# A fused three-layer transformer on one core: batch 0's q and k a tick earlier in the lead-in, and the modulations of two layers given out in smaller pieces

## The chip, the cores and the metric

The kernel runs on one core of a Trainium2 chip. A core has five engines that work side by side, each with its own queue of instructions that it takes in order: TensorE (PE in the profile; its weight loads are shown apart as PEld), VectorE (DVE), ScalarE (ACT), GpSimd (POOL) and SyncE (SP), which here issues nearly all transfers. An engine stops at an instruction until the instructions that it depends on, on other engines or in the DMA queues, are done, and everything behind it in its queue waits as well. The metric is the device time of one execution in microseconds.

## The reference

32 sequences ("batches") of 128 tokens with 144 channels, and one condition vector of 144 for each, pass through four layers:

```python
x = _L0_cond_ref(x, cond, ...)   # attention (q and k normalised per head), MLP
x = _L1_cond_ref(x, cond, ...)   # x + (z R - z) U^T, z = x U
x = _L2_cond_ref(x, cond, ...)   # attention, MLP
x = _L3_cond_ref(x, cond, ...)   # attention, mixture of 4 experts, top 2
```

Layers 0, 2 and 3 have 16 heads of 9 channels. Their normalised input is modulated, `ln(x) * (1 + scale) + shift`, and the result of attention and of the MLP is multiplied by a gate before it is added to x. Shifts, scales and gates come from the condition: `silu(c) @ w_mod + b_mod`, 144 to 6 x 144, a matrix for each of the three layers. Layer 0 also normalises q and k over the 9 channels of each head:

```python
q = _ln(q, g_q); k = _ln(k, g_k)      # mean and variance over 9 channels, then a learnt factor
attn = softmax(q @ k^T * 9 ** -0.5)
```

Layer 1 needs U, the orthogonal factor of a QR decomposition of P (144 x 64), and for each batch R = expm(A), where the 64 x 64 skew matrix A is filled from `silu(cond) @ W.T + b`. Neither depends on x.

## The kernel before

The three attention layers are numbered 0, 1 and 2 in the code (the rotation by U and R is done between 0 and 1). A fixed schedule, written out by hand, sets the order of all instructions: a loop over *ticks* from -6 on, and in each tick a row of named places, *gaps*: a, e, t, first half of the scores, stats, b0, b, den, pre1, second half of the scores, c, y1, y2, y3, d, z. In tick b of layer 0 the first scores of batch b are computed, in tick b + 1 its softmax weights, in tick b + 2 its sums and its projection. `put(tick, gap, f)` lays a piece of work into a gap; `fill(tick, gap)` gives it out. Ticks -6 to -1 are the lead-in. The kernel uses eight PSUM banks for what TensorE writes; one is kept for the attention outputs, and `bank()` hands out the other seven in rotation, so a matmul can wait for the engine that reads what the bank held seven banks ago.

Around the change lie these pieces:

- `modulations(n)` (L263 to L283): shifts and scales of layer n for all batches, 40 small matmuls into one bank (8 with 128 output rows, c < 4, and 32 with 32 rows, at L274) and four copies on DVE (L278 to L281) into modM and modR. `ln_T` (L652 to L655) transposes a normalised batch and applies modM and modR on ACT.
- `layer_gates(n)` (L285 to L300): the gates of layer n, four matmuls (L291), a copy on ACT (L296) and two writes to DRAM by SP (L298). `load_gates` (L305) brings them back, spread over 128 partitions, once per four batches.
- `first_gates` (L1178): layer_gates(0), then the loads of the last layer's modulation weights into the place that layer 0's held. `without_means` (L1170 to L1176): DVE takes the mean over each head out of the q and k weights, in place.
- Layer 0's q and k, batch by batch: `qk0_project` (L686, L687 on TensorE, a copy and a square on ACT, L741, L742), `qk0_variance` (a sum on DVE, L747; scaling on POOL, L748), `qk0_guess` and three `qk0_newton` (an inverse square root, L754 to L767; on DVE for batch 0, on POOL else), `qk0_divide` (DVE, L771) and `qk0_T` (four transposes, L783, and three copies on ACT, L786 to L788, into qT and kT, which the scores read).
- `prep_qr`: the QR decomposition, 64 columns one after another. Each column is a loop through the engines: TensorE spreads a row (L327), ACT squares and copies it (L338, L340), POOL takes a root (L339), DVE makes the reflection (L342 to L349) and applies it to the matrix `at` (L353), which the next column's matmul reads. `prepare_qr` gives out one column per tick in the lead-in and two per tick afterwards.
- `prep_expm`: the matrix exponential as a generator of many steps. Before: modulations and gates of layer 1 (one step), of layer 2 (one step), then the first half of A (matmuls L414 with the weights W4, copy on ACT L420), its transposition (`ps_at`, L429, and a product on DVE, L434), the second half, its transposition, the row sums and the scaling, the powers, the series and the squarings. Each half of A reads four tiles of W4; the second four are loaded (L189) into the same places once the first half has been computed. A branch (L585, L586) follows the first four squarings: further ones are computed only if a norm asks for it, which it does not here. All engines go through the branch.
- `prepare_expm` (L1208): gives out one step of `prep_expm` in gap z of tick -2, and from tick 0 on one in gap b and one in gap z of each tick.

## Time and profile before

| | us |
|---|---|
| three runs | 1311.20, 1311.47, 1315.63 (median 1311.47) |
| profiled execution | 1311.55 |
| its span, first to last instruction | 1309.8 |
| TensorE busy | 1264.6 (97%) |
| DVE / ACT / POOL busy | 799.4 / 833.1 / 701.9 |
| scores of batch 0 start | 40.47 |
| the branch | 323 |

A line of the profile's order of time gives start, duration, engine, source line, operation, the tiles written and read, shapes and count, and in brackets how long the engine had been idle and what ended that. Matmuls overlap, so their durations are longer than the distance from one to the next; an f32 matmul appears as two records. PEq, DVEq, SPq are the sequencers of the engines. Windows give the busy time of PE, PEld, DVE, ACT and POOL in a stretch, then the TensorE clock that was granted (1.00 is full), the mean share in which the DMA engines were busy, and GB/s.

### The profile page before, as it was taken

The page shows a single profiled execution, that of the slowest core. Times are in us where ns is not written, and L with a number is a line of the kernel's source. Part 1 is how long each engine was busy: PE and PEld are TensorE (multiplying, and loading weights), DVE is VectorE, ACT ScalarE, POOL GpSimd, SP SyncE. Part 2 cuts the span into 40 slices and gives each one's busy share as a digit, 9 for nine tenths or more (in the row PEclk, how much of TensorE's full clock was granted, in tenths as well). Part 3 has the DMA queues.
Part 4 walks back from the last instruction along what each step waited for, and adds up shares of the span by engine and source line. Part 5 has one row for each costly group of instructions (what it writes and reads, how often), then busy time and mean ns, then how long its engine had stood idle before and what let it go on. Part 6 is the DMA issues. An engine that isn't in the chain of part 4 may idle for free.

```text
span 1309.8 us, 35666 instructions
## 1 busy us (share of the span) xinstructions
PE 1264.6 (97%) x14180; PEld 924.2 (71%) x14180; DVE 799.4 (61%) x2516; ACT 833.1 (64%) x1832; POOL 701.9 (54%) x1691
## 2 busy tenths in 40 slices
PE   6889898999989999999999999999999999999997
PEld 5678686787776667667677767767676767677665
DVE  5698888876864456666666666646464646454322
ACT  2567768678757566777767777665656565555431
POOL 5667777765744444445545454746464646351632
PEclk9999999999989999999999999999999999999999
DMA  8200000000003000000110000200000000000000
GB/s 231 62 2 21 20 2 20 20 3 22 20 2 134 19 11 21 11 20 20 36 29 20 20 11 11 76 11 19 11 20 11 19 11 19 11 19 2 19 10 10
DMA packets 21671, 34.43 MB, mean 26 GB/s; under 512 B 2304, under 2 KB 12448, under 8 KB 21248
## 3 DMA queue, kind: packets, MB, share of 16 engines
q1 hardware_dynamic: 20848, 31.70, 8.1%
q8 instruction: 114, 1.87, 0.6%
q10 hardware_dynamic: 656, 0.42, 0.2%
q14 instruction: 53, 0.43, 0.1%
HBM read 29.65 MB, written 2.47 MB: 25 GB/s over the span
## 4 chain that ended last, share of the span: by engine, by line
PE 71%; DVE 2%; ACT 1%; POOL 0%; issue 0%; POOLq 0%; DVEq 0%
PE ps_h L665 19%; PE ps_f L1109 10%; PE ps_s L853 7%; PE ps_qk L665 6%; PE ps_w L853 6%; PE ps_o L880 5%; PE ps_f L974 5%; PE ps_pj L944 3%; PE ps_v L665 2%; PE ps_f L1114 1%; PE ps_o L812 1%; PE ps_cw L1097 1%; DVE nm L858 1%; PE ps_hT_m L652 1%; PE ps_hT_m L653 1%; PE ps_z L1006 1%
## 5 line engine op out<-in xcount | busy, mean ns | idle before, releaser
L858 DVE TENSOR_REDUCE nm<-ps_s 128x4 f32<-128x512 f32 x384 | 246.2, 682 | 90.1 <-PE ps_w L853 68.4
L865 ACT ACTIVATE pr<-ps_w 128x512 f32<-128x512 f32 x384 | 208.6, 595 | 104.0 <-PE ps_w L853 102.5
L853 PE MATMUL ps_s<-kT,qT 32*128 32x256 f32 x1536 | 227.8, 404 | 0.7 <-ACT kT L788 0.6
L853 PE MATMUL ps_w<-q,kT 32*128 32x128 f32 x3072 | 228.2, 282 | 0.0
L853 PEld LDWEIGHTS ps_w<-q,kT 32*128 32x128 f32 x3072 | 193.4, 187 | 9.8 <-issue 6.2
L968 ACT ACTIVATE hid<-ps_h 128x512 f32<-128x512 f32 (+1 forms) x224 | 119.5, 591 | 100.4 <-PE ps_h L665 99.9
L853 PEld LDWEIGHTS ps_s<-kT,qT 32*128 32x128 f32 x1536 | 134.5, 184 | 30.0 <-issue 8.9
L665 PE MATMUL ps_h<-hM_m,mlps 128*128 128x512 f32 x304 | 144.0, 607 | 0.0
L1118 DVE SCALAR_TENSOR_TENSOR acc<-ps_f,cw,acc 128x144 f32<-128x144 f32 x128 | 46.6, 365 | 152.3 <-PE ps_f L1114 73.5
L930 POOL TENSOR_TENSOR x_sb<-x_sb,res_a 128x144 f32<-128x144 f32 x96 | 47.1, 490 | 147.1 <-DVE res_a L933 146.4
L880 PE MATMUL ps_o<-pr,vaug 128*32 128x128 f32 x3072 | 104.1, 276 | 0.0
L880 PEld LDWEIGHTS ps_o<-pr,vaug 128*32 128x32 f32 x3072 | 78.1, 109 | 32.5 <-PE ps_w L853 18.9
L665 PEld LDWEIGHTS ps_h<-hM_m,mlps 128*128 128x128 f32 x304 | 53.3, 189 | 67.6 <-issue 66.6
L731 POOL TENSOR_SCALAR kT<-kT,cst 128x512 f32<-128x512 f32 x40 | 62.4, 1565 | 61.5 <-ACT kT L718 60.5
L974 PE MATMUL ps_f<-mlps,hid 128*128 128x144 f32 x640 | 94.8, 296 | 0.0
L974 PEld LDWEIGHTS ps_f<-mlps,hid 128*128 128x128 f32 x640 | 83.5, 193 | 7.6 <-issue 3.4
L865 ACT ACT_TABLE_LOAD x57 | 73.1, 1283 | 6.5 <-PE ps_w L853 5.7
L626 POOL TENSOR_SCALAR rs_m_a<-mv_m_a 128x2 f32<-128x2 f32 x81 | 15.6, 193 | 114.4 <-DVE mv_m_a L624 86.0
L655 ACT ACTIVATE hM_m<-ps_hT_m,modM 128x128 f32<-128x128 f32 x96 | 44.7, 465 | 50.5 <-PE ps_hT_m L653 50.4
L965 ACT ACT_TABLE_LOAD x58 | 74.4, 1283 | 1.0
L1109 PEld LDWEIGHTS ps_f<-pair,hid 128*128 128x128 f32 x512 | 66.9, 190 | 8.4 <-issue 7.7
L1109 PEld LDWEIGHTS ps_f<-mlps,hid 128*128 128x128 f32 x512 | 66.7, 190 | 8.2 <-issue 6.9
(324 smaller groups left out, 2931.1 us busy)
## 6 DMA issues: line engine op xcount, KB each, us to landing
gates<-gates SPq DMA_DIRECT2D x48, 288.0 KB, 3.5
x_sb<-in_x SPq DMA_DIRECT2D x8, 288.0 KB, 9.4
out_x<-x_sb SPq DMA_DIRECT2D x8, 288.0 KB, 2.5
mlps<-in_L_mlp SPq DMA_DIRECT2D x2, 1000.0 KB, 5.8
pair<-in_L_mlp SPq DMA_DIRECT2D x1, 1800.0 KB, 9.7
mlps<-in_L_mlp SPq DMA_DIRECT2D x1, 1800.0 KB, 8.2
pow<-in_W SPq DMA_DIRECT2D x4, 320.0 KB, 6.8
mlps<-in_L_wmod SPq DMA_DIRECT2D x4, 290.0 KB, 4.8
```

The lines of the kernel that those rows point to most:

```text
L665: nc.tensor.matmul(ps, x, y, start=k == 0, stop=k == 1)
L731: eng.tensor_scalar(o, k, m, None, ALU.mult)
L853: nc.tensor.matmul(o, x, y, start=True, stop=True)
L858: nc.vector.tensor_reduce(nmv[:, at0 : at0 + 2, ONE : ONE + 2], view.rearrange("p (r t k) -> p r t k", t=2, k=T), AX.X, ALU.max, negate=True,)
L865: nc.scalar.activation(pr[:, 4 * e : 4 * e + 4, :].rearrange("p s q -> p (s q)"), view, AF.Exp, scale=SCALE,)
L880: nc.tensor.matmul(po[rows4(j), t, :], v[:, 4 * j + 2 * t + r, :], prs[j // 2][:, 4 * (j % 2) + 2 * r + t, :], start=r == 0, stop=r == 1,)
L930: nc.gpsimd.tensor_tensor(x_sb[:, b, :], x_sb[:, b, :], t, ALU.add)
L965: nc.scalar.activation(t, half, AF.Gelu_apprx_tanh)
L968: nc.scalar.activation(hid[:n, i], ps[:n], AF.Gelu_apprx_tanh)
L974: nc.tensor.matmul(ps, hid[:, at0, i, :], w2[:, m, :], start=m == 0, stop=m == NFC - 1)
L1109: nc.tensor.matmul(ps[:, 0, :], hid[:, at0 + m, i, :], w2[:, at0 + m, :], start=m == 0, stop=m == 3)
L1118: nc.vector.scalar_tensor_tensor(acc, ps[:, 0, :], w, acc, ALU.mult, ALU.add)
```

## The change

The lead-in of layer 0 is ordered anew, and the step generator's first steps are cut smaller and given out at more places.

- `modulations(n)` computes its two parts one after the other, each into a bank of its own and each followed by its two copies; it is a generator now, with a step for each part. `prep_expm` has six steps for layers 1 and 2 (two parts and the gates each) where it had two.
- `prepare_expm` gives out nothing in the lead-in any more. In ticks 0 and 1 it gives out a step in each of the gaps b0, b, c, y2 and z; from tick 2 on in b and z, as before. Ten steps are therefore given out by the end of tick 1: the six above, the first half of A (tick 1, b), its transposition (c), the second half (y2) and its transposition (z). Before, that point was reached in tick 2, b. From tick 2 on every step of the exponential stands one gap earlier than before, the branch among them (tick 23, b, where it stood in tick 23, z).
- Batch 0's q and k are projected in tick -4 instead of -3, guessed and refined in tick -3 (on DVE, as before), divided at the end of tick -3 and transposed in tick -2.
- `first_gates` moves from tick -4 to tick -2, `without_means` from the end of tick -4 to gap t of tick -5.
- The scaling in `qk0_variance` goes to DVE for batches 0 to 3 and stays on POOL for the others.

```diff
     def modulations(n):
         w = w_mods[n]
-        mm = const.tile([128, 4, B], F32, name=f"modM{n}")
-        mr = const.tile([128, 4, B], F32, name=f"modR{n}")
-        ps = bank([128, 8, B], f"ps_mod{n}")
-        for c in range(8):
-            at0 = (c % 4) * (CM + 32)
-            for r in range(1 if c < 4 else 4):
-                m, at1 = (CM, at0) if c < 4 else (32, at0 + CM)
-                for k in range(2):
-                    rows = slice(0, KH + k)
-                    nc.tensor.matmul(
-                        ps[32 * r : 32 * r + m, c, :], w[k][rows, at1 : at1 + m], csT[rows, k, :],
-                        start=k == 0, stop=k == 1,
-                    )
-        nc.vector.tensor_copy(mm[:, :2, :], ps[:, :2, :])
-        nc.vector.tensor_scalar_add(mm[:, 2:, :], ps[:, 2:4, :], 1.0)
-        nc.vector.tensor_copy(mr[:, :2, :], ps[:, 4:6, :])
-        nc.vector.tensor_scalar_add(mr[:, 2:, :], ps[:, 6:8, :], 1.0)
-        modM.append(mm)
-        modR.append(mr)
+        for part, mods in enumerate((modM, modR)):
+            t = const.tile([128, 4, B], F32, name=f"mod{'MR'[part]}{n}")
+            ps = bank([128, 4, B], f"ps_mod{n}_{part}")
+            for c in range(4):
+                at0 = c * (CM + 32) + part * CM
+                m = 32 if part else CM
+                for r in range(4 if part else 1):
+                    for k in range(2):
+                        rows = slice(0, KH + k)
+                        nc.tensor.matmul(
+                            ps[32 * r : 32 * r + m, c, :], w[k][rows, at0 : at0 + m], csT[rows, k, :],
+                            start=k == 0, stop=k == 1,
+                        )
+            nc.vector.tensor_copy(t[:, :2, :], ps[:, :2, :])
+            nc.vector.tensor_scalar_add(t[:, 2:, :], ps[:, 2:, :], 1.0)
+            mods.append(t)
+            yield
...
         for n in (1, 2):
-            modulations(n)
+            yield from modulations(n)
             layer_gates(n)
             yield
...
-    def qk0_variance(s):
+    def qk0_variance(s, eng):
         va = small.tile([128, 32], F32, tag="qkv", name=f"qkv_{s}", bufs=2)
         nc.vector.tensor_reduce(va, st[s].pop("sq"), AX.X, ALU.add)
-        nc.gpsimd.tensor_scalar(va, va, 1.0, EPS, ALU.mult, ALU.add)
+        eng.tensor_scalar(va, va, 1.0, EPS, ALU.mult, ALU.add)
...
-        if prep_expm and (tick >= 0 and gap in ("b", "z") or (tick, gap) == (-2, "z")):
+        if prep_expm and tick >= 0 and gap in (("b0", "b", "c", "y2", "z") if tick < 2 else ("b", "z")):
             said = next(prep_expm, 0)
...
                 if layer == 0:
-                    put(t0 + i - 3, "c", qk0_project, s)
-                    put(t0 + i - 3, "z", qk0_variance, s)
-                    put(t0 + i - 2, "e", qk0_guess, s)
-                    if s == 0:
+                    early = s == 0
+                    put(t0 + i - 3 - early, "c", qk0_project, s)
+                    put(t0 + i - 3 - early, "z", qk0_variance, s, nc.vector if s < 4 else nc.gpsimd)
+                    put(t0 + i - 2 - early, "e", qk0_guess, s)
+                    if early:
                         for gap in "bbc":
-                            put(-2, gap, qk0_newton, s, nc.vector)
+                            put(-3, gap, qk0_newton, s, nc.vector)
+                        put(-3, "z", qk0_divide, s)
+                        put(-2, "b0", first_gates)
+                        put(-2, "b", qk0_T, s)
                     else:
                         for gap in ("b", "c", "y2"):
                             put(t0 + i - 2, gap, qk0_newton, s)
-                    put(t0 + i - 1, "b", qk0_divide, s)
-                    put(t0 + i - 1, "c", qk0_T, s)
+                        put(t0 + i - 1, "b", qk0_divide, s)
+                        put(t0 + i - 1, "c", qk0_T, s)
...
-    put(-5, "b", modulations, 0)
-    put(-4, "b", first_gates)
-    put(-4, "z", without_means)
+    put(-5, "b", lambda: list(modulations(0)))
+    put(-5, "t", without_means)
```

## The prediction

> **What bounds the kernel now.** I read the page's table of engines and its 40 slices first, then the windows of the first 90 us, then the order of time on TensorE, DVE and the DMA queue from 10 to 84 us, last the waits around the branch at 323 us. All numbers are us of the one profiled execution: span 1309.8, time 1311.55 (1.75 outside the span); the median of the three runs is 1311.47, so a sum made on the execution stands for the median as well. Three runs spread over 4.4 us, so 0.5%, 6.6 us, is about what can be told from no change.

> ```profile
> PE 1264.6 (97%) x14180; PEld 924.2 (71%) x14180; DVE 799.4 (61%) x2516; ACT 833.1 (64%) x1832; POOL 701.9 (54%) x1691
> ...
> PE 71%; DVE 2%; ACT 1%; POOL 0%; issue 0%; POOLq 0%; DVEq 0%
> ```

> TensorE is busy nearly all the time. The chain that ended last can be followed back to 323.15, the branch, and is TensorE throughout, so what the start of the program loses or gains is carried to the end. The windows (x counts; the last columns are granted clock, DMA share, GB/s) show where the edited stage is bound:

> ```profile
> 35.00:40.00 5.00, 2.96 (x9) 2.41 (x10) 1.69 (x7) 1.20 (x3) 4.07 (x15) 1.00 0.20 62
> 40.00:45.00 5.00, 5.00 (x38) 4.23 (x36) 3.62 (x14) 2.33 (x9) 3.82 (x13) 1.00 0.01 2
> 55.00:60.00 5.00, 4.76 (x71) 3.41 (x65) 4.86 (x12) 4.23 (x14) 4.09 (x15) 1.00 0.99 234
> 60.00:70.00 10.00, 9.93 (x146) 6.52 (x140) 7.51 (x25) 5.89 (x18) 5.72 (x19) 1.00 0.03 8
> 70.00:80.00 10.00, 6.99 (x97) 5.36 (x97) 9.17 (x35) 5.05 (x17) 6.15 (x18) 0.94 0.01 2
> ```

> Up to 40 us TensorE has holes; in 40 to 70 (ticks 0, 1 and most of 2) it is full; in 70 to 80 DVE is the bound. In order of time:

> ```profile
> 33.40 0.42 PE L652 MATMUL ps_hT_a<-cst,xh_a 128*128 128x128 f32 x1
> 37.04 1.09 PE L783 MATMUL ps_qkT<-cst,qkn 128*128 128x128 f32 x4 [3.01 <-DVE qkn L771]
> 40.47 1.50 PE L853 MATMUL ps_s<-kT,qT 32*128 32x256 f32 x8
> 42.98 0.27 PE L652 MATMUL ps_hT_a<-cst,xh_a 128*128 128x128 f32 x1
> ...
> 54.41 0.56 SPq L189 DMA_DIRECT2D wt<-in_W  x1
> ...
> 60.63 0.11 PEld L414 LDWEIGHTS ps_a<-wt,csT 72*32 72x32 f32 x1 [0.98 <-DMA wt<-in_W]
> ...
> 77.00 0.51 PE L327 MATMUL ps_qr<-at,cst 128*128 128x145 f32 x2 [1.78 <-DVE at L353]
> ...
> 323.29 0.73 PE L944 MATMUL ps_pj<-L_wproj,oT 128*128 128x144 f32 x4 [1.07 <-DVEq L586]
> ```

> and the windows behind the wait at 77.00, with the granted clock third from the end:

> ```profile
> 78.00:79.00 1.00, 1.00 (x22) 0.81 (x17) 0.96 (x4) 0.18 (x2) 0.79 (x4) 0.90 0.00 0
> 79.00:80.00 1.00, 1.00 (x8) 0.78 (x7) 0.86 (x4) 0.62 (x2) 0.96 (x3) 0.50 0.00 0
> ...
> 82.00:83.00 1.00, 1.00 (x7) 0.67 (x7) 0.90 (x5) 0.47 (x3) 0.47 (x2) 0.90 0.00 0
> ```

> The reader sees: the scores of batch 0 start at 40.47; TensorE ran at half speed until then (the same transpose takes 0.42 at 33.40 and 0.27 at 42.98, though the granted clock reads 1.00); the second product of the exponential (L414) already waits 0.98 for its weights W4; an idle of 1.78 is followed from 78.8 to 82.2 by a granted clock of 0.50; and the branch costs TensorE 1.07.

> **The change part by part.**

> *1. Lead-in.* Layer 1's modulations and gates leave it (26.45 to 32.75, 6.3 at half speed), and batch 0's q and k chain runs a tick earlier, but it now lies on DVE between two steps of the QR, which is the loop of the lead-in. Walking the new order with the rows of before: tick -5 keeps its times. The centring of the weights (L1170 to L1176, 18.91 to 21.37, 2.46) moves ahead of its QR step: 10.5 to 12.9, its weights having landed at 9.0 (issued 4.34, 4.7 to landing); the QR step then ends 14.7, under the modulations of layer 0, which hold TensorE to 15.3. Tick -4: q and k of batch 0 stand where the first gates stood, 17.2 to 19.3; ACT squares to 20.1, DVE's variance to 20.75, guess and statistics to 21.6, QR step to 23.35. Tick -3: three Newton steps on DVE (27.16 to 29.79, 2.63) and the division (0.45) end at 26.4; the next QR step waits behind them and ends 28.65, not 27.2. Tick -2 on TensorE: QR 23.4, first gates to 26.5, then the transposes of batch 0, q and k of batch 1 to 29.8. Tick -1: QR on DVE 32.3 to 34.05. So QR of tick 0 starts at 34.1 and the scores 0.63 later (39.84 to 40.47), at 34.7: **-5.75**. Ends: -7 if one QR turn (3.6 to 4.4) shrinks to its chain, -3 if a queue adds a wait in two ticks.

> *2. What comes back in tick 0.* The 40 matmuls of layer 1 and its four gate matmuls (counted before splitting into records) cost what layer 2's cost at full speed, 43.20 to 46.68: **+3.48**, on an engine without holes there. Six steps instead of two, but the same matmuls and DVE copies (0.23 and 0.21 each, beside TensorE); one more bank each, no instruction.

> *3. POOL and DVE at tick 0.* POOL must finish batch 1's Newton steps (3.83 for three, behind the statistics chain) before QR's square root: 38.1, 3.4 after the scores; in before 1.2 after. DVE's maxima and with them the banks of the second scores come about 0.8 late: **+0.8** (0 to 2). The variance's scaling for four batches goes from POOL (0.22) to DVE (0.18 by the same shape's row): nothing, DVE idles 3.93 before 40.83.

> *4. The W4 loads.* This is the largest loss. In before the two halves of the exponential's input stand a tick apart (tick 0 and tick 1, gap z). In after, five steps of tick 0 and one of tick 1 go to modulations and gates, and both halves fall into tick 1, gaps b and y2. The second half's weights overwrite the first's, so their four loads are issued when the first is done (51.74) and the last is there at 60.63: 8.89 later, with the DMA engines at 0.99 share and 234 GB/s, so by bandwidth. Between the halves TensorE will have QR 0.60, scores 1.34, transposes 0.49, q and k 0.97, ps_at 1.21: 4.61. It waits 4.28 in place of the 1.12 by which the second half is now longer (59.50 to 62.47 against 49.89 to 51.74): **+3.15** (0 if other waits fill it, 4.3). Behind the waiting matmuls stand the maxima's transpose (L812), so DVE's q and the next tick's weights. The second ps_at (L429) now follows at once and waits for ACT's copy of 0.59: **+0.6**. On SP the last gate writes stand ahead of the W4 loads as before; their data is ready 2 earlier (ACT's copy behind the exponentials, 4 into tick 1; the first half ends 6 into it), so they add nothing. The first gates' own transfers on SP (two writes, two weight loads of 290 KB, 24.03 to 26.25) move to about 27 to 29.5 and, with 4.8 to landing, are there at 34, some 10 before the modulations that read them: nothing.

> *5. Clock.* TensorE will idle 1.1 (at half speed) to 2.5 (at full) before tick 0 and 4.28 in tick 1. The nearest row is the idle of 1.78 and the 3.4 at 0.50 behind it, half of which is lost: 1.7. I take **+1.7** twice (each from 0; the first up to 6.8, see the second rival).
> [...]

> *6. The branch.* The expm chain ends one step earlier, and the branch moves from gap z to gap b of tick 23. There TensorE is done at 314.4, and DVE's last instruction ahead of the branch (qkn, 316.04 + 0.49) and its own load and compare (about 0.8) end at 317.3: 2.9 of idle in place of 1.07, **+1.8**. Ends 0 and 3.4 (TensorE's compare-and-branch alone lasts 3.40, covered now by matmuls). The other steps of the chain change places between b and z, two to a tick as before; bound +-2, taken as 0.

> Sum: -5.75 + 3.48 + 0.8 + 3.15 + 0.6 + 3.4 + 1.8 = +7.5. 1311.55 + 7.5 = **1319.0**.

> **The rivals.** (a) *DVE, not TensorE, sets ticks 0 to 3; not slower.* For it: DVE has 9.17 of 10 in 70 to 80, and TensorE idles 1.14, 1.78 and 0.38 there and loses 1.7 by the clock, 5.0 in all. Then items 2 and 4 and the second clock loss (8.9) hide: 1310.1. It decides once DVE has no idle of its own at the start of tick 2; in before it idles 2.11 at 62.0 to 64.15, which speaks against it. If the first clock loss and the branch are free too (3.5) it ends at 1306.6; if item 3 (0.8) and the half clock of 79 to 82 (1.7) go as well, at 1304.1, and with the lead-in's far end at 1302.8.
> (b) *Half speed lasts through tick 0.* For it: TensorE stayed at half speed from 10 to 40 us in before, dense as it was. The three pieces of modulations and gates (5.9 at full speed) and first scores and values (2.5) take 1.81 times as long (6.3 against 3.48): 6.8 in place of 1.7, 1324.1. Against it: 26.5 to 33 is dense with full matmuls in the new order, and in before 2.9 of such (37.04 to 39.9) came just ahead of full speed.
> (c) *The lead-in gives less*, since QR waits behind the Newton steps twice: -3, 1321.7.

> **How the numbers follow.** Forecast 0.46, (a) 0.34 (some 0.3 of that in its low end), (b) and (c) together 0.20. The forecast's own range is 1314 to 1325 and lies above 1318.1 in seven cases of ten: 0.32 slower, 0.14 same. (a) gives 0.10 faster, 0.21 same and, with the upper ends of clock and branch, 0.03 slower; (b) and (c) are slower. Slower 0.55, same 0.35, faster 0.10. The range 1306 to 1327 leaves out the low end of (a) and the upper tail of (b), some 0.16.

> **What would show it.** First ps_s near 34.7 (item 1; over 38 refutes it); a wait of L412 on the load of W4 near 4 in tick 1 (item 4); granted clock 0.50 behind it or matmuls at 0.42 in tick 0 (item 5, b); start of tick 3's scores some 5 to 6 later than 72.55 (items 1 to 5; at or before 72.55 speaks for (a)); an idle near 2.9 at the branch (item 6). The prediction is wrong if that wait is short, or if TensorE's idle of 70 to 84 is gone.

## The result and the profile after

The changed kernel takes 1327.32 us (median of 4 runs, 1325.94 to 1334.47), the kernel before 1311.34 on the same chip (4 runs, 1308.31 to 1315.63): a ratio of 1.0118, 95% interval 1.0081 to 1.0156. It is slower, by 1.2%. The profiled execution has a span of 1324.0 and a time of 1325.94, 14.1 and 14.39 more than before; the working below is on these two executions. The forecast was 1319.0 with a range of 1306 to 1327: the sign holds, the size is about half of what was measured (7.5 for 14.39 in the profiled execution and 15.5 by the ratio), and the median lies at the upper end of the range, 0.3 above it.

From here on, lines of the changed kernel's file behind the modulations are two lower than in the kernel before (L414 is now L412, L858 is L856).

The page of the changed kernel, engines and granted clock in 40 slices of 33 us:

```profile
PE 1271.1 (96%) x14180; PEld 928.6 (70%) x14180; DVE 799.5 (60%) x2520; ACT 832.4 (63%) x1832; POOL 698.6 (53%) x1687
...
PEclk8789998999999999999999999999999999999999
```

The first slices are below 9. The first slice of the kernel before reads 9, which tells nothing: its record of the clock begins at 41.2 (last section), while of the two transposes of a batch the second starts 0.21 after the first at 33.40 and 0.11 after it at 42.98. The windows of the changed kernel (us from the start, busy time of PE, PEld, DVE, ACT, POOL with instruction counts, then granted clock, DMA share, GB/s):

```profile
35.00:40.00 5.00, 5.00 (x24) 3.99 (x22) 1.31 (x8) 0.55 (x3) 3.92 (x16) 0.50 0.00 0
40.00:45.00 5.00, 5.00 (x80) 4.44 (x80) 3.16 (x12) 1.24 (x4) 2.24 (x8) 0.51 0.00 0
50.00:55.00 5.00, 5.00 (x101) 4.17 (x101) 3.37 (x18) 2.33 (x5) 1.80 (x5) 0.67 0.04 11
60.00:70.00 10.00, 8.53 (x77) 3.48 (x70) 4.00 (x12) 3.65 (x11) 2.46 (x9) 1.00 0.64 162
70.00:80.00 10.00, 8.63 (x132) 6.58 (x132) 8.70 (x29) 6.00 (x18) 6.12 (x20) 1.00 0.01 2
```

In 35 to 45, the first part of tick 0, TensorE is busy throughout and runs at a clock of 0.50; in 60 to 70 it waits while the DMA engines are at 0.64. In order of time on TensorE (start, length, line, tiles; in brackets the idle time before it and what ended it):

```profile
27.06 1.11 PE L781 MATMUL ps_qkT<-cst,qkn 128*128 128x128 f32 x4 [0.48 <-DVE qkn L769]
...
34.49 0.76 PE L325 MATMUL ps_qr<-at,cst 128*128 128x145 f32 x2 [2.14 <-DVE at L351]
35.19 2.08 PE L851 MATMUL ps_s<-kT,qT 32*128 32x256 f32 x8
...
42.69 0.42 PE L650 MATMUL ps_hT_a<-cst,xh_a 128*128 128x128 f32 x1
...
57.17 0.62 PE L412 MATMUL ps_a<-pow,csT 72*32 72x512 f32 x2
57.18 0.62 PE L412 MATMUL ps_a<-hid,csT 72*32 72x512 f32 x1
57.19 0.62 PE L412 MATMUL ps_a<-wt,csT 72*32 72x512 f32 x1
...
63.23 1.04 PE L412 MATMUL ps_a<-pow,csT 72*32 72x512 f32 x2
64.78 1.04 PE L412 MATMUL ps_a<-pow,csT 72*32 72x512 f32 x2 [0.51 <-DMA pow<-in_W]
66.14 1.05 PE L412 MATMUL ps_a<-hid,csT 72*32 72x512 f32 x2 [0.32 <-DMA hid<-in_W]
67.41 0.62 PE L412 MATMUL ps_a<-wt,csT 72*32 72x512 f32 x1 [0.22 <-DMA wt<-in_W]
...
69.25 0.33 PE L810 MATMUL ps_nm<-cst,nm 128*128 128x128 f32 x1
69.99 1.16 PE L427 MATMUL ps_at<-cst,hid 128*64 128x64 f32 x32 [0.42 <-ACT hid L418]
...
86.76 0.82 PE L325 MATMUL ps_qr<-at,cst 128*128 128x145 f32 x2 [2.06 <-DVE at L351]
...
330.90 0.48 PE L325 MATMUL ps_qr<-at,cst 128*128 128x145 f32 x2 [3.22 <-PEq L584]
```

The wait of qkT in the lead-in, 3.01 before, is 0.48, and batch 0's scores start at 35.19 (40.47 before). Then the scores last 2.08 and a transpose 0.42; at a clock of 1.00 they last 1.13 (at 45.02) and 0.27 (at 56.86). The second half of the exponential's products (63.23 to 69.25) lasts 6.02 in place of 2.97, with its bracketed waits all on the loads of W4. Those waits add up to only 1.05. The rest is lost because products no longer run side by side: in the first half four start within 0.02 of each other (57.17 to 57.19), in the second the first three start one by one, at 63.23, 64.78 and 66.14, as their tiles land. The branch costs TensorE 3.22 in place of 1.07. The lag of the changed kernel against the kernel before, taken at the maxima's transpose of each tick (ps_nm), is 0.90 in tick 0, 9.95 in tick 1, 8.86 in tick 2, 9.44 in tick 10, 13.30 in ticks 17 to 22, 16.89 in tick 23, 15.9 in ticks 25 to 27 and 14.7 from tick 29.

### The profile page after: what moved, and what is told of

Read it like the earlier page. It is cut to its first block, busy times and chain, and to the rows that moved or that the text cites. A ratio compares the mean times of both kernels' runs of the same rounds, so it can differ in the third digit from the quotient of the medians.

```text
span 1324.0 us, 35670 instructions
## 1 busy us (share of the span) xinstructions
PE 1271.1 (96%) x14180; PEld 928.6 (70%) x14180; DVE 799.5 (60%) x2520; ACT 832.4 (63%) x1832; POOL 698.6 (53%) x1687
## 4 chain that ended last, share of the span: by engine, by line
PE 70%; DVE 3%; ACT 1%; POOL 0%; issue 0%; POOLq 0%; DVEq 0%
PE ps_h L663 19%; PE ps_f L1107 9%; PE ps_s L851 7%; PE ps_qk L663 6%; PE ps_w L851 6%; PE ps_o L878 5%; PE ps_f L972 5%; PE ps_pj L942 3%; PE ps_v L663 2%; PE ps_f L1112 1%; PE ps_o L810 1%; DVE nm L856 1%; PE ps_cw L1095 1%; PE ps_z L1004 1%; PE ps_hT_m L651 1%; PE ps_hT_m L650 1%
## 5 line engine op out<-in xcount | busy, mean ns | idle before, releaser
L856 DVE TENSOR_REDUCE nm<-ps_s 128x4 f32<-128x512 f32 x384 | 246.4, 683 | 95.6 <-PE ps_w L851 73.9
L851 PE MATMUL ps_s<-kT,qT 32*128 32x256 f32 x1536 | 231.3, 409 | 0.6 <-ACT kT L786 0.6
L878 PEld LDWEIGHTS ps_o<-pr,vaug 128*32 128x32 f32 x3072 | 78.0, 109 | 32.3 <-PE ps_w L851 18.9
L624 POOL TENSOR_SCALAR rs_m_a<-mv_m_a 128x2 f32<-128x2 f32 x81 | 15.5, 191 | 114.6 <-DVE mv_m_a L622 86.2
```

Source lines behind the costliest of these rows:

```text
L851: nc.tensor.matmul(o, x, y, start=True, stop=True)
L856: nc.vector.tensor_reduce(nmv[:, at0 : at0 + 2, ONE : ONE + 2], view.rearrange("p (r t k) -> p r t k", t=2, k=T), AX.X, ALU.max, negate=True,)
L878: nc.tensor.matmul(po[rows4(j), t, :], v[:, 4 * j + 2 * t + r, :], prs[j // 2][:, 4 * (j % 2) + 2 * r + t, :], start=r == 0, stop=r == 1,)
```

## The experiments

All were compared with the kernel before on the chip where they ran; its median was 1310.88 (13 runs) for the lead-in, pieces, own-places and fill runs, 1312.64 (13 runs) for the three with wide operands and the branch run, 1312.01 (29 runs) for the next three (everything taken away, fillers alone, first combination) and 1312.77 (17 runs) for the last. "At tick 2" means the position of that tick's ps_nm against the kernel before, in the profiled executions.

### Half the change: the lead-in alone, the pieces alone

The lead-in run has the new lead-in, but gives out a layer's modulations and gates in one step at the old places; the pieces run has the old lead-in with the pieces at five places.

```
e3_lead (against the changed kernel)
-            yield from modulations(n)
+            list(modulations(n))
...
-        if prep_expm and tick >= 0 and gap in (("b0", "b", "c", "y2", "z") if tick < 2 else ("b", "z")):
+        if prep_expm and (tick >= 0 and gap in ("b", "z") or (tick, gap) == (-2, "z")):
```

```
e4_pieces (against the changed kernel; qk0_variance, qk0_newton, qk0_divide and qk0_T likewise)
-                    put(t0 + i - 3 - early, "c", qk0_project, s)
+                    put(t0 + i - 3, "c", qk0_project, s)
...
-    put(-5, "t", without_means)
+    put(-4, "b", first_gates)
+    put(-4, "z", without_means)
```

> The changed kernel with only its lead-in order kept: modulations and gates of layers 1 and 2 are one step each again, the first in tick -2, gap z, and steps come in gaps b and z as before. Theory (the loss comes from what the smaller pieces move into ticks 0 and 1: the W4 wait, half clock there, the branch at gap b): no such wait, branch at gap z, scores of batch 0 at 39 to 42, time 1309 to 1315. Rival (the reordered lead-in itself costs, by QR behind the Newton steps and by clock): scores at 43 or later, 1318 or more.

> The changed kernel with the old lead-in order put back (q and k of batch 0 in ticks -3 to -1, first gates in tick -4, centring of the weights at the end of tick -4) and the pieces in five gaps kept. Theory: the W4 wait of about 4, half clock in ticks 0 and 1 and the branch at gap b are all there: 1322 to 1330. Rival (the new lead-in order is what costs): 1309 to 1315.

Measured: lead-in alone 1308.35 (10 runs), ratio 1.0003 (0.9967 to 1.0039); pieces alone 1331.44, ratio 1.0155 (1.0108 to 1.0201). Both times lie just outside the theory's ranges (0.65 below and 1.4 above) and far from the rival's. The lead-in costs nothing that can be told, the pieces cost all. What they cost is seen in the windows of the pieces run:

```profile
50.00:55.00 5.00, 5.00 (x103) 4.44 (x105) 2.39 (x14) 1.45 (x5) 0.92 (x3) 0.80 0.05 11
55.00:60.00 5.00, 5.00 (x29) 3.95 (x26) 3.19 (x11) 2.25 (x4) 2.92 (x9) 0.50 0.03 7
60.00:65.00 5.00, 5.00 (x25) 1.42 (x27) 0.00 (x0) 1.82 (x5) 0.00 (x0) 0.50 0.00 0
65.00:70.00 5.00, 5.00 (x36) 3.73 (x38) 1.29 (x2) 2.82 (x9) 2.46 (x9) 0.50 0.86 218
```

From 53.0 to 70.0 the clock is halved, though TensorE has not waited: it is busy 5.00 of 5.00 in each window, the one ahead of the half clock included. My explanation of item 5, idle time, cannot be the cause here.

### The wait for W4 taken away

The second half of W4 gets places of its own (four of the tiles hid, and rotU) and is loaded behind the x tiles, so nothing has to be waited for.

```
-        wt = mat(f"wt{c}", ("pow3", "pow4", "even_lo", "odd_lo")[c % 4])[:KP]
+        tags = ("pow3", "pow4", "even_lo", "odd_lo", "w4_4", "w4_5", "w4_6", "w4_7")
+        wt = mat(f"wt{c}", tags[c])[:KP]
...
-            if t == 0:
-                for c in range(4, 8):
-                    load_W4(c)
             yield
```

> The changed kernel with places of their own for the second half of W4 (the MLP's hidden tile and the tile of the rotated U, unused until later), loaded behind the x loads at the start, so that nothing waits for the first half. Theory: no wait on W4, the second half takes 1.9 in place of 6.0, tick 2 starts 4.2 earlier than in the changed kernel, time 1321 to 1324. Rival (the wait only takes the place of DVE waits in ticks 2 and 3): tick 4 within 1 of the changed kernel, 1325 to 1328.

Measured: 1327.14, ratio 1.0122 (1.0072 to 1.0173); nothing gained, the theory's 1321 to 1324 is missed. In its trace the wait is gone, in order of time on TensorE:

```profile
69.08 0.62 PE L424 MATMUL ps_a<-hid,csT 72*32 72x512 f32 x2
...
70.41 0.60 PE L424 MATMUL ps_a<-rotU,csT 73*32 73x512 f32 x2
70.94 0.33 PE L819 MATMUL ps_nm<-cst,nm 128*128 128x128 f32 x1
```

The second half takes 1.86, but it starts at 69.08 in place of 63.23: its windows show why.

```profile
55.00:60.00 5.00, 5.00 (x23) 3.13 (x25) 1.61 (x4) 1.84 (x6) 1.30 (x5) 0.50 0.21 64
60.00:65.00 5.00, 5.00 (x38) 2.50 (x30) 0.00 (x0) 1.14 (x4) 1.19 (x4) 0.50 0.01 3
```

The clock, halved from 51.7 to 55.1 in the changed kernel, stays halved from 51.0 to 68.0 here. The 4.2 that the wait gives free go there. So the run does not say that the wait was harmless; it says that in this execution another loss of the same size took its place.

### What halves the clock

Four runs go after it. The fill run puts filler matmuls (the identity against itself, 128 by 128, results not read) into TensorE's waits ahead of tick 0. The wide run leaves the waits and changes the modulations and gates: the condition vectors are repeated four times, so that the modulations M stream 128 columns and the gates hold 128, in the same number of matmuls; the extra results are not read. The third does both, the fourth puts the wide operands into the lead-in run.

```
e5_fill
+    put(-3, "z", warm, 6)
+    put(-1, "z", warm, 9)

e6_wide
+    csW = pp.tile([KH + 1, 2, 4 * B], F32, name="csW")
+    csT = csW[:, :, :B]
...
-                            ps[32 * r : 32 * r + m, c, :], w[k][rows, at0 : at0 + m], csT[rows, k, :],
+                            ps[32 * r : 32 * r + m, c, :], w[k][rows, at0 : at0 + m], csW[rows, k, :wide],
...
-                    psg[:, c, :], csT[rows, k, :], w[k][rows, MODC + c * C : MODC + (c + 1) * C],
+                    psg[:, c, :], csW[rows, k, :], w[k][rows, MODC + c * C : MODC + (c + 1) * C],
```

The third run, e7_widefill, has both sets of lines; the fourth, e8_leadwide, is e3_lead with the lines of e6_wide.

> The changed kernel plus 15 matmuls of the identity with itself, 128x128, into the attention output's bank, which nothing reads then: 6 at the end of tick -3 and 9 at the end of tick -1, where TensorE idles 3.07 and 2.14. Theory (half clock in tick 0 follows from that idle and costs most of what the sum missed): granted clock 1.00 from about 31 to 45, the maxima's transpose of tick 0 at 46 instead of 50.55, time 1320 to 1323.5. Rival (the work moved into tick 0 costs by itself, clock or not): within 1.5 of the changed kernel's 1326 to 1327, or slower by the added 2.

> The changed kernel with the condition vectors repeated four times side by side: the modulations M stream 128 columns (32 before) and the gates hold 128 columns (32 before) on TensorE; the extra results are not read. The number of matmuls is the same, and a 128-column matmul lasts 0.11 in the traces, like the 32-column ones (0.45 for 4 at full speed). Theory 'array use': the clock is halved behind a stretch of some 3.4 in which the matmuls fill little of TensorE's array, whether it waits or runs small matmuls; then the half clock of 38.0 to 44.85 and of 51.68 to 55.09 in the changed kernel goes or shrinks, worth 2.5 to 4.5, at 1322.5 to 1325 (the wait of 2.14 ahead of tick 0 stays, so 34.6 to 38.0 may stay at half). Theory 'idle' (item 5: the clock is halved by TensorE's waits alone): no change, 1326.5 to 1328.

> The wide operands and the fillers of the fill run together (6 and 9 filler matmuls of 128 by 128 in TensorE's waits of ticks -3 and -1). Theory 'array use': with neither the wait nor the small matmuls ahead of and in tick 0, the half clock of 34.6 to 44.85 goes as a whole, 5 to 6.5 in all against the changed kernel: 1320.5 to 1322.5, while fillers alone gave 1328.92 and the wide operands alone less. Theory 'idle': as the fill run, 1327 to 1330.

> The lead-in run (changed lead-in; modulations and gates of a layer in one step as before) with the wide operands. Its half clock of 34.0 to 37.4 follows 3.4 of modulations and gates without any wait, that of 44.2 to 51.05 another such stretch. Theory 'array use': both go, worth 2.5 to 4 against the lead-in run's 1308.35: 1304 to 1306, faster than the kernel before by 0.3 to 0.5%. Theory 'idle': no change, 1307.5 to 1309.5.

Measured: fill 1328.92 (ratio 1.0136, 1.0087 to 1.0184); wide 1326.01 (1.0115, 1.0068 to 1.0162); both 1325.83 (1.0105, 1.0067 to 1.0143); lead-in with wide operands 1308.89 with the kernel before at 1312.64 (0.9977, 0.9948 to 1.0006). As times, all four miss the range of their theory, and the fill run and the lead-in run with wide operands end in that of the rival. By the time alone the wide operands gain nothing in the lead-in run either (1308.89 with them, 1308.35 without, on different chips). What decides is in the traces, one execution of each. The fill run, in order of time on TensorE:

```profile
31.26 2.17 PE L1342 MATMUL warm<-cst 128*128 128x128 f32 x18
33.39 0.51 PE L325 MATMUL ps_qr<-at,cst 128*128 128x145 f32 x2
33.83 1.13 PE L851 MATMUL ps_s<-kT,qT 32*128 32x256 f32 x8
```

and by windows:

```profile
34.00:38.00 4.00, 4.00 (x32) 3.62 (x33) 0.68 (x4) 0.55 (x3) 3.09 (x13) 0.91 0.00 0
38.00:42.00 4.00, 3.74 (x75) 2.98 (x76) 3.44 (x14) 1.89 (x7) 3.40 (x11) 0.50 0.02 4
42.00:46.00 4.00, 4.00 (x15) 2.56 (x11) 2.82 (x11) 1.21 (x3) 2.21 (x9) 0.50 0.00 2
```

The fillers take the place of the wait of 2.14 and delay nothing, and the scores run at full speed (1.13). Three microseconds later, behind scores and modulations without any wait, the clock is halved all the same, from 37.3 to 47.5. The windows of the lead-in run from 39 to 51:

```profile
39.00:42.00 3.00, 3.00 (x28) 2.70 (x24) 0.35 (x3) 1.17 (x4) 2.34 (x10) 1.00 0.03 8
42.00:45.00 3.00, 2.46 (x78) 2.05 (x78) 2.45 (x9) 0.39 (x1) 2.56 (x9) 0.87 0.00 0
45.00:48.00 3.00, 3.00 (x13) 1.89 (x13) 1.55 (x7) 0.55 (x3) 2.17 (x8) 0.50 0.05 12
48.00:51.00 3.00, 3.00 (x12) 1.84 (x14) 2.50 (x10) 1.64 (x5) 0.93 (x4) 0.50 0.00 0
```

And the same windows of the lead-in run with wide operands:

```profile
39.00:42.00 3.00, 3.00 (x57) 2.88 (x57) 0.39 (x3) 1.17 (x4) 2.33 (x10) 1.00 0.00 0
42.00:45.00 3.00, 2.80 (x69) 2.40 (x58) 2.83 (x10) 0.81 (x4) 2.61 (x8) 1.00 0.00 0
45.00:48.00 3.00, 3.00 (x24) 1.76 (x24) 2.69 (x11) 1.84 (x6) 2.38 (x9) 1.00 0.05 12
48.00:51.00 3.00, 3.00 (x40) 1.74 (x33) 2.19 (x12) 1.74 (x6) 0.82 (x3) 1.00 0.14 22
```

The only difference in the code is the width of the operands (with three small copies on ACT that make them), and the half clock of 44.2 to 51.05 is gone; at tick 3 the run stands 2.0 ahead of the kernel before, the lead-in run 1.45 behind it.

With all traces in hand it can be put in numbers for these executions. In each trace the clock changes at whole multiples of one length, 3.413 (in the changed kernel at 24.37, 34.61 and 51.68: 3 and 5 lengths apart). I cut the 14 profiled executions into these stretches and counted for each, from the records of the matmuls that start in it, the streamed columns weighted by the share of the 128 rows and 128 columns that the matmul uses (a 128 by 128 transpose counts 128; at full speed the next starts 0.11 after it, at 56.86 and 56.97). These weighted columns are the "columns" below, my measure for what the expectations call array use:

```
kernel            stretch from   clock  TensorE busy  columns  clock of the next
changed           31.20          1.00   0.37          1297     0.50
changed           34.61          0.50   1.00           730     0.50
changed           38.02          0.50   1.00           650     0.50
changed           41.44          0.50   1.00          1556     1.00
changed           48.26          1.00   1.00           914     0.50
lead-in           40.81          1.00   0.98           689     0.50
lead-in, wide     39.96          1.00   1.00          1876     1.00
fill              33.86          1.00   1.00          1250     0.50
fill and wide     34.78          1.00   1.00          2105     1.00
```

Without the first recorded stretch and the end of each trace, 5120 such stretches were at full clock and 61 of them were followed by half clock. Over these, "below 1460 columns" misjudges 11 of the 5120, the best limit on TensorE's busy time (0.53) misjudges 23. The two weights together do best: with the share of the columns alone the best limit misjudges 16, with the share of the rows alone 28, with the streamed columns unweighted 41. The limit was fitted behind the measurement, some records are missing from the traces, and exceptions remain (the kernel before from 44.66: 1292 columns, and full clock behind it). At half clock the same work takes longer (the scores 2.08 for 1.13), so fewer columns fall into a stretch. Of the 111 half stretches all 19 with fewer than 1250 columns were followed by another, of the 47 with 1640 or more only one was, and between them both happen. In the run without W4's wait the five half stretches from 51.0 count 1354, 1131, 1487, 1323 and 1792. One pair of executions could owe its difference to how the stretches fall; so all of them: half clock behind a stretch with TensorE busy for over 0.97 is seen in each of the six executions with narrow operands in the new lead-in or in pieces (seven stretches), and in none of the six with wide ones.

Why fill and wide together gained nothing: tick 0 now ends 1.84 ahead of the kernel before (0.90 behind in the changed kernel), but W4's second half comes no earlier. On TensorE:

```profile
59.11 1.02 PE L416 MATMUL ps_a<-pow,csW 72*32 72x512 f32 x2
60.69 1.05 PE L416 MATMUL ps_a<-pow,csW 72*32 72x512 f32 x2 [0.56 <-DMA pow<-in_W]
63.18 1.91 PE L416 MATMUL ps_a<-hid,csW 72*32 72x512 f32 x2 [1.45 <-DMA hid<-in_W]
```

The second half now lasts from 59.11 to 67.62, 8.5, and behind the waits (58.7 to 62.1 counts 416 columns) the clock is at half from 62.1 to 72.3. At tick 2 the run is 8.38 behind, the changed kernel 8.86.

### The branch

```
             yield from square_all(t)
+        yield
         n_more = nc.values_load(more, min_val=0, max_val=1)
```

> The changed kernel with one empty step more in the chain of the exponential, so that the branch stands in gap z of tick 23 again and the steps behind the modulations in the gaps that they had before. Theory (item 6): the branch's wait of 3.22 at 330.9 shrinks to about 1.07 and the half clock behind it goes, together 2.6 to 3.6 as the tick marks of the two traces show: 1323.5 to 1325. Rival: the place of the branch costs nothing by itself, the time behind tick 25 is taken up again: 1326.5 to 1328.

Measured: 1329.00, ratio 1.0140 (1.0098 to 1.0181). The trace shows the theory's step and the time does not: TensorE waits 1.07 at the branch, as the theory said,

```profile
340.15 0.73 PE L943 MATMUL ps_pj<-L_wproj,oT 128*128 128x144 f32 x4 [1.07 <-DVEq L585]
```

no half clock follows it, and from tick 22 to tick 25 the run's lag stays between 16.97 and 16.74, where the changed kernel's goes from 13.30 to 16.89 and then 15.9. But this execution came to tick 22 with 3.7 more lag, which it had by tick 2 (12.95 for 8.86): from 31 on its clock was at half from 34.9 to 48.6, 52.0 to 55.4 and 69.1 to 79.3, four stretches more than in the changed kernel by then. The branch's 2.6 (3.6, of which 1.0 is made up by tick 25) are therefore gone in this trace, and hidden by the clock of its start; by the time alone the run is a miss. Nor does gap z keep the clock whole by itself, as the next run shows.

### Everything taken away at once

The changed kernel with fillers, wide operands, W4's own places and the branch in gap z.

> The changed kernel with everything that the runs so far blame taken away at once: wide operands and fillers (no half clock ahead of and in tick 0), places of their own for the second half of W4 (no wait in tick 1), one empty step (the branch in gap z again). The first two each saved nothing in total when alone: without the wait the clock stayed at half from 51 to 68, and with the clock full TensorE came to the wait of W4 earlier. Theory 'three terms, each hiding behind another': the maxima's transpose of tick 2 stands at +0 to +2 against the kernel before (changed kernel +8.86, wide and filled +8.38), the branch adds nothing, and the time is 1311 to 1314.5. Rival 'something else of the pieces costs, DVE or POOL': +4 or more stay at tick 2, and the time is 1317 to 1322.

Measured: 1319.16 (10 runs, 1311.74 to 1330.83), ratio 1.0065 (1.0031 to 1.0099), 7.0 less than the changed kernel by the ratios, 8.2 by the medians; the profiled execution took 1315.1. The time misses the theory's 1311 to 1314.5 and lies in the rival's range; the place at tick 2 is 0.1 beyond the theory's +2 and short of the rival's +4. At tick 2 it stands 2.11 behind the kernel before, where the changed kernel has 8.86, the run without W4's wait 10.56 and the one without the half clock 8.38. On TensorE between the two halves of W4 there is no wait on a load left; the first that is left behind them is ACT's copy:

```profile
63.23 1.16 PE L440 MATMUL ps_at<-cst,hid 128*64 128x64 f32 x32 [0.45 <-ACT hid L434]
```

So up to tick 2 the W4 wait and the half clock each hid behind the other, 6.75 together in this pair of executions. The branch did not keep to the theory: it stands in gap z of tick 23 as in the kernel before, and yet costs 1.43 of waiting and two half stretches behind it (326.6 to 333.5), which take the lag from 2.83 at tick 23 to 6.38 at tick 24; 3.63 are left from tick 29.

```profile
326.48 1.16 PE L956 MATMUL ps_pj<-L_wproj,oT 128*128 128x144 f32 x4 [1.43 <-DVEq L598]
```

About half of the loss is thus removed by taking away what was blamed; the other half, 7 to 8.5, is not. It goes with the clock, which still differs from run to run: the spans of the ten runs go with the mean granted clock, 1310.0 at 0.992 to 1329.1 at 0.978 (correlation of span and half-clock time 0.98, 0.46 lost per us at half clock). What makes the clock of one run fall where that of another does not was not tried.

### Toward a faster version

Three runs use what was found. The first is the kernel before with fillers alone in five of the QR's six longest waits of ticks 3 to 28. The other two are the lead-in run with wide operands, W4's own places and these fillers; in the last the W4 loads are issued at the end of tick -1, and the fillers of the fill run are added.

```
e11_stalls (against the kernel before)
             ps = bank([128, C + 1], f"ps_qr{j}")
+            for _ in range({13: 12, 29: 13, 37: 16}.get(j, 0)):
+                nc.tensor.matmul(ps[:, :128], ident, ident, start=True, stop=True)
...
(10 and 7 such matmuls ahead of ps_yr and ps_uT)

e12_best2 (against e8_leadwide): the same QR fillers, the places of e1_own, the fillers of e5_fill
+    put(-1, "z", lambda: [load_W4(c) for c in range(4, 8)])
```

> The kernel before with 12, 13 and 16 filler matmuls of 128 by 128 ahead of the 14th, 30th and 38th column of the QR, and 10 and 7 behind its end (at 77.0, 163.2, 213.7, 378.4 and 379.9 of its trace), where TensorE waits 1.2 to 2.4 for DVE; fillers of 0.11 each fit into the waits. Theory 'array use': the half clock at 78.8, 164.1 and 379.2 to 386 (four stretches of 3.41, each worth 0.7 to 1.6) goes: 1307 to 1309.5 with the kernel before at 1311.4, a ratio of 0.9965 to 0.9985. Rival 'the fillers delay the columns that they stand ahead of': 1311 to 1313.

> The lead-in run with wide operands (1308.89 with the kernel before at 1312.64), with places of their own for the second half of W4 and the fillers in the QR's waits. Theory 'array use': 1 from the wait of W4 and 2 to 3 from the half clock that is left (its trace has 3 stretches of it, 162.8 and 377.9 to 384.7), the two kept by a clock that is full: 1303 to 1306 with the kernel before at 1311.4, a ratio of 0.9940 to 0.9965, faster than both kernels. Rival: the gains hide behind DVE in ticks 2 to 4, 1308 to 1310.

> The run before this one (lead-in of the change, modulations and gates in one step, wide operands, places of its own for the second half of W4, fillers in the QR's waits) with two things changed: the four loads of W4's second half are issued at the end of tick -1, behind the first gate writes, since in that run ACT's copy of the gates waited 6.87 for those writes (they stood behind the loads on the DMA queue) and the scores came at 42.91 in place of 37.46; and the fillers of the fill run stand in the waits of ticks -3 and -1. Theory: the scores come near 37.5 again, no wait for W4 (1 less than in the kernel before), full clock from some 30 on: 1304 to 1307.5 with the kernel before at 1311.5 to 1312, a ratio of 0.9930 to 0.9970. Rival: the loads at the end of tick -1 hold up the second gate writes or the gates' loads of tick 0, and the time is 1309 to 1312.

Measured: fillers alone 1316.15, ratio 1.0012 (0.9983 to 1.0042); the first combination 1310.75, ratio 0.9984 (0.9956 to 1.0012); the second 1306.46 (12 runs, 1305.31 to 1308.83), ratio 0.9959 (0.9936 to 0.9982). The fillers alone miss both ranges, the first combination ends just above its rival's, and the second is where its theory put it: 0.4% faster than the kernel before, a small gain. The first combination missed by a queue, as ACT in its lead-in shows:

```profile
38.93 0.39 ACT L311 COPY gsb<-ps_gate 32x288 f32<-32x288 f32 x1 [6.87 <-DMA gates<-gsb]
39.23 0.28 ACT L354 ACTIVATE qrk<-ps_qr 128x145 f32<-128x145 f32 x1
```

The first gate writes stood behind the four W4 loads on SP, and QR's square stood behind the gates' copy on ACT. With the loads behind the writes, and with the fillers, the second combination stands 3.40 ahead of the kernel before at tick 2 and 5.06 from tick 29, and its clock reads 9 in each slice of the page (mean 0.997):

```profile
PEclk9999999999999999999999999999999999999999
```

The fillers in the kernel before removed all but one half-clock stretch (91.1 to 94.5 is left) and gained 1.6 between tick 10 and tick 29; what that run lost it lost at its start, which the last section takes up.

## Why the prediction was right on the sign and short on the size

*Item 1, the lead-in.* Predicted -5.75, measured -5.28 (35.19 for 34.7). Right within 0.5; the pieces run and the lead-in run show that this part is not where the loss is.

*Item 2, the moved work.* Predicted +3.48; at full speed it is 1.80 for M (in the fill run), 0.78 for R and 1.10 for the gates, 3.7. Right as work at full speed, but the changed kernel runs the modulations of layer 1 (M and R) at half speed.

*Item 3, POOL and DVE in tick 0, +0.8.* No sign of it: TensorE does not wait between 35.19 and 63.23. Where tick 0 runs at full speed, the term appears: with everything taken away QR waits 0.81 for DVE at 41.45. In the changed kernel, at a clock of 0.50 until 44.85, it does not show.

*Item 4, W4 and at1.* Predicted +3.15 and +0.6, measured +3.05 (6.02 for 2.97) and +0.42. Right in mechanism and size: the second half is 4.16 longer than the 1.86 that it takes without the wait, for the 4.28 that I had worked out, though only 1.05 of it stands in brackets as idle. What the step did not say is that the price is a place in time, not a length: in the filled and wide run, where tick 0 ends 1.84 ahead of the kernel before, the second half lasts 8.5 for 6.02.

*Item 5, the clock.* This step failed, in what it took to halve the clock and so in its size. It priced idle time, 1.7 behind the wait ahead of tick 0 and 1.7 behind W4's. At the start of tick 2 (QR's matmul at 71.08 for 62.47) the lag is 7.45 without the 1.16 of the second ps_at, which the kernel before does later; less items 1, 2 and 4 (-5.28, 3.48, 3.05, 0.42) 5.8 are left, in place of 3.4. They lie at 34.6 to 44.85 and 51.7 to 55.1. The first follows the wait of 2.14, but in the fill run, without that wait, half clock came behind the scores and modulations all the same (from 37.3); the second follows modulations, with no wait at all. And behind W4's wait, where I put 1.7, the clock stayed whole (65.3 to 68.7 counts 872 columns, one of the exceptions to the limit). Rival (b), half speed through tick 0, is nearer to what happened: clock 0.50 from the start of tick 0 to 44.85, the scores at 2.08 for 1.13 and the transposes at 0.42 for 0.27, and full clock for the rest of the tick, layer 1's gates among it. Its sum, 1324.1, is 1.8 below the profiled execution's 1325.94; that it comes so near is in part luck, since the later half stretches are not in it. I held it unlikely on the ground that 26.5 to 33 is dense; dense was the wrong measure: the stretch from 27.8, with q and k products and transposes, counts 1954 columns and full clock follows it, while those from 34.6 and 38.0, with scores and modulations, count 730 and 650 and the one from 48.3, with modulations and gates, 914, and half clock follows each.

*Item 6, the branch.* Predicted +1.8 with 3.4 as the far end; measured 3.6 at tick 23 and 2.6 from tick 25, of which the wait itself is 2.15 (3.22 for 1.07). The wait of 3.22 is ended by TensorE's own queue: its compare-and-branch lasts 3.37 and starts at 327.2, uncovered. I had walked DVE's way to the branch (2.9) and taken it as the limit; TensorE's own compare-and-branch, which I had named for the far end, was. Behind it comes one half stretch, 331.6 to 335.0, which the step left out.

*Not in the prediction:* 2.0 from the start of tick 2 to tick 10, 1.4 of it in tick 2, where TensorE now waits for DVE at 74.56 and 79.03 (0.48 and 0.33); and 3.9 in ticks 11 to 17. The waits there are QR's waits on DVE: 2.45 in tick 11 (1.92 in the kernel before) and 2.43 in tick 15 (2.44 in the kernel before). That the first is longer by 0.5 goes with the exponential's steps in other gaps, a term that I had set to 0 within 2; nothing of it is left at tick 14 (9.38). The second is the same wait, but in the changed kernel two half stretches follow it and in the kernel before none. From tick 14 to tick 17 the lag grows by 3.9 to 4.0 in the five kernels with the pieces that have two half stretches there, by 2.66 in the two that have one, and by 1.08 in the one that has none: so some 2.8 of the 3.9 are the clock, and 1.1 is something else that was not looked for. How the stretches fall on such a wait may decide; half clock behind both waits was seen in seven of the eight kernels with the pieces, and in none of the three that have neither the pieces nor fillers in the QR's waits. Why so regularly is open; it was not tried.

*Rival (a), DVE hides it:* refuted. The lag at tick 10 (9.44) is not less than at tick 2 (8.86), tick 3's scores start 8.84 later than before (81.39 for 72.55; I had said 5 to 6), and the waits on DVE in ticks 3 to 15 are still there.

*Rival (c), the lead-in gives less:* refuted by item 1.

Over the whole profiled execution: 9.4 by tick 10, 3.9 in ticks 11 to 17, 2.6 at the branch, -1.2 at the end of the QR (one half stretch in place of two), -0.6 behind it, together 14.1, which is the difference of the spans. Without the clock, the terms of the first three ticks and the wait at the branch (-5.28, 3.7, 3.05, 0.42, 2.15) make 4.0, less than the 6.6 that I had called the least that can be told from no change: that the sign came out clearly is owed to the half clock, which the sum had too small.

## What to carry to other kernels

Ask of small matmuls not only how long they last but how many rows and columns they use and stream: here some 3.4 us of them in a row were followed by 3 to 17 us at half speed, with TensorE busy for over 0.97 of the time by the profile, and behind operands widened to 128 columns, at the same 0.11 per record, no such stretch was seen. When two losses lie one behind the other, removing either alone may show no gain; remove both before calling one harmless. A step moved past a load that reuses a buffer is priced by when that buffer is free (3.05 here), so first give the load a place of its own, and then look at what stands behind it on its queue.

## What the runs showed of the hardware that I had not expected

The start cost the fillers-alone run more than its trace's clock tells. In these traces the granted clock reads 1.00 until its first change is recorded (in the fillers-alone run from 40 to 60 throughout); that run, whose first change is at 56.94, shows it on TensorE:

```profile
40.96 2.08 PE L860 MATMUL ps_s<-kT,qT 32*128 32x256 f32 x8
...
52.56 2.08 PE L860 MATMUL ps_s<-kT,qT 32*128 32x256 f32 x8
```

The scores take 2.08, as at a clock of 0.50 in the changed kernel (35.19), and full speed is seen from 57 on, where a transpose lasts 0.27 (57.17); in the profiled execution of the kernel before the first recorded stretch at full speed starts at 41.2. With the fillers alone tick 1 is 7.48 late for this reason. It fits that the span hardly goes with the granted clock's half time in the kernel before (correlation 0.41 over 29 runs, spans of 1305.2 to 1321.5) and closely in the lead-in run (0.99 over 10 runs): there the first full speed comes at 30.6 and is recorded. That the spread of the kernel before comes from its start is argued from this, not shown run by run. The last version, with fillers in the lead-in, has the narrowest spread of those with ten runs or more, 3.5.
